# The causal mask of the transposed scores: a minimum by VectorE in the PSUM bank for a product by TensorE

## The chip, the cores and the metric

The kernel runs on one core of one Trainium2 chip. The metric is device time in microseconds (us) of one execution; less is better. The engines are named as in the profile: PE (TensorE matmul), PEld (its weight loads), DVE (VectorE), ACT (ScalarE), POOL (GpSimd) and SP (SyncE, which issues most transfers). [...]

## What is computed

A small model of six layers over `x` of 4 batches, 512 positions and 128 features, each layer added to its input:

```python
x = x + 0.5 * ffn0(layernorm(x))      # tree-routed q, k, v, one attention head of 128
x = x + attn0(layernorm(x))           # causal attention, 16 heads of 8
x = x + 0.5 * ffn0(layernorm(x))
x = x + 0.5 * ffn1(layernorm(x))      # 8 experts, 2 taken, and a shared one
x = x + attn1(layernorm(x))           # a Mamba block: a scan over the positions
x = x + 0.5 * ffn1(layernorm(x))
```

The change lies in the second layer, the attention with 16 heads:

```python
scores = jnp.einsum('bhqd,bhkd->bhqk', q, k) / math.sqrt(Dh)
scores = scores + _alibi_slopes(H)[None, :, None, None] * rel[None, None]
causal = jnp.triu(jnp.ones((S, S), dtype=bool), k=1)
scores = jnp.where(causal[None, None], jnp.float32(-1000000000.0), scores)
attn = jax.nn.softmax(scores, axis=-1)
out = jnp.einsum('bhqk,bhkd->bhqd', attn, v)
```

## The kernel before

**Jobs.** Every layer of every batch is a few Python generators, called jobs. A table of due times (`TIMES`) says when each job's steps are to be traced, and the loop at the end of `macaron` always takes the step that is due first. A list scheduler of the framework then orders the traced instructions of each engine, by that priority and by when their inputs and buffers come free in its own reckoning, and puts in all semaphores. So the order in which an engine works is fixed when the kernel is compiled, and each engine takes its instructions strictly in that order. Layers of different batches overlap: while one batch is in the 16-head attention, another is in a tree layer or with the experts.

**Buffers.** `bank(role)` takes a PSUM bank from a ring of its role (`BANKS`); `head_sc` has two, `head_max` one, `tree_mm` three. `work(role)` takes an SBUF tile from a ring (`BUFS`).

**The 16-head attention of one batch** (names starting with `head_`) runs over u = 0, 1 and g = 0, 1, four heads at a time:

- `head_prep`, `head_stack`: norm, q, k, v with the rotary embedding, written by DMA into stacks `q_bias` and `k_bias` whose extra rows carry the position bias.
- `head_keys` (L541): POOL makes four masked copies `km` of the keys, one for each head of the group.
- `head_scores`: PE makes scores with queries on the partitions (L557, bank `head_max`). One custom DVE instruction for each head (L565) takes the minimum of minus the score and the causal mask `future`, and keeps the negated row maximum. It works in place in the bank, and an accumulator read follows it.
- `head_maxima` (L579 to L584): the negated maxima are turned, split in two and written by DMA into rows of `q_bias`, so that the next product subtracts them.
- `head_mix`: scores once more, now transposed, with keys on the partitions (L633, bank `head_sc`), for one block `kt` of 128 keys and the queries from that block on: 512, 384, 256 or 128 columns for each head. A bank holds 1, 1, 2 or 4 heads, so there are 4 + 4 + 2 + 1 = 11 groups for each (u, g), and 16 x 11 = 176 groups in all. The first 128 query columns of each head meet the diagonal and need the mask. Before, this is one more product into the same bank: the identity `ident_h` as weights, and the mask `future_t` (0, or -2^100 where the key comes after the query) as moving operand, in bf16 and broadcast over the heads of the bank (L641). ACT then takes the exponential of the whole bank into a tile `pt` (L649, six tiles). Four groups later (`LAG_MIX`) PE multiplies `pt` by the values (L601, bank `head_acc`).
- `head_end`: projection and residual (L668, L669).

Other lines that the text names: `mm3` (L173 to L175) is a product of split operands in three matmuls, for the tree layers (`tree_mm`), the experts (`moe`), the scores of the tree layers' own attention (`attend`) and others; L394 is the tree layers' ReLU with the routing mask on DVE; L404 their second product; L318 a transposition on PE; L353 and L355 make the routing masks, with `leafpath` as weights; L438 is a row maximum of `attend`; L740 is part of the experts' routing; L972 is the scan of the Mamba block.

The constants are one array, `whole`, which a DMA of ACT's queue loads once at the start: `leafpath`, `ident_h`, `future_t` (128 columns each), and `future` (512 columns) for L565.

Of the kernel before, what the change touches and what calls it, by code (L numbers as in the profile page):

```python
# [17 lines left out]
BF16 = mybir.dt.bfloat16  # L18
# [3 lines left out]
ALU = mybir.AluOpType  # L22
AX = mybir.AxisListType

P = 128
B, S, D = 4, 512, 128
# [48 lines left out]
FAR = 2.0**100  # L75
# [37 lines left out]
def macaron(ctx: ExitStack, tc: tile.TileContext, t: dict, stages: int = 6):  # L113
    nc = tc.nc
# [6 lines left out]
    def bank(role):  # L121
        return psum.tile([P, S], F32, tag=role, name=role, bufs=BANKS[role])
# [4 lines left out]
    def tiny(shape, tag, bufs=2):  # L127

        n = int(np.prod(shape[1:]))
        if tag not in turns:  # L130
            first = taken_of[0]
            taken_of[0] += bufs * n
            assert taken_of[0] <= SCRATCH
            turns[tag] = cycle([scratch[:, first + n * i : first + n * i + n] for i in range(bufs)])
        out = next(turns[tag])
        if len(shape) == 2:
            return out
        names = "abcd"[: len(shape) - 1]
        sizes = dict(zip(names, shape[1:]))
        return out.rearrange(f"p ({' '.join(names)}) -> p {' '.join(names)}", **sizes)  # L140

    def work(role, shape=(S,), dtype=F32):

        return wp.tile([P, *shape], dtype, tag=role, name=role, bufs=BUFS[role])
# [19 lines left out]
    def load_split(name, src, shape, alloc_hi, alloc_lo, engine, by=None):  # L164
        raw = work("stage", shape)
        engine.dma_start(out=raw, in_=src)
        split(alloc_hi, alloc_lo, raw, by)
        return raw
# [13 lines left out]
    def keep(n):  # L182
        nonlocal cut
        cut += n
        assert cut <= KEPT
        return kept[:, cut - n : cut]
# [10 lines left out]
        rounded[:, (2 + TREES) * D + k * EXPERTS : (2 + TREES) * D + (k + 1) * EXPERTS] for k in (0, 1)  # L197
    ]
    load_split("nodes", t["nodes"], [P], *nodes, nc.scalar)
    whole = keep((3 * P + S) // 2).bitcast(BF16)  # L200
    nc.scalar.dma_start(out=whole, in_=t["whole"])
    leafpath, ident_h, future_t = (whole[:, ts(k, P)] for k in range(3))
    future = whole[:, 3 * P :]


    at = {}
# [108 lines left out]
    def transposed(src, role):  # L315
        ps = bank(role)
        for i in range(NT):
            nc.tensor.transpose(ps[:, ts(i, P)], src[:, ts(i, P)], ident)  # L318
        return ps
# [270 lines left out]
    def head_mix(b, st, consts, u, g):  # L590

        vv = consts()[2][0]
        km, qs = st.km[u, g], st.qs[u]
        if (u, g) == (0, 0):
            st.o = work("o")
        acc = bank("head_acc")

        def mix(kt, prob):
            for j in range(4):
                h = u * HALF + 2 * j + g  # L600
                nc.tensor.matmul(  # L601
                    acc[32 * j : 32 * j + 32, kt * P :],
                    lhsT=vv[:, b % 2, kt, h * (HD + 1) : h * (HD + 1) + 32],
                    rhs=prob[j],
                    start=(kt == 0),
                    stop=(kt == NT - 1),
                )

        mixed = []

        def take():
            mixed.append(work("mixed"))
            nc.scalar.copy(mixed[0], acc)

        def turn():
            ps = transposed(mixed[0], "head_turn").rearrange("p (n j c) -> p n j c", n=NT, j=4)
            rden = tiny([P, NT, 4], "rden")
            nc.vector.reciprocal(rden, ps[:, :, :, HD])
            view = st.o.rearrange("p (n u j g d) -> p n u j g d", n=NT, u=2, j=4, g=2)
            nc.vector.tensor_mul(  # L620
                view[:, :, u, :, g, :],
                ps[:, :, :, :HD],
                rden.unsqueeze(3).to_broadcast([P, NT, 4, HD]),
            )

        for kt in range(NT):
            n = S - kt * P
            prob = []
            each = (1, 1, 2, 4)[kt]
            for j0 in range(0, 4, each):  # L630
                view = bank("head_sc")[:, : each * n].rearrange("p (h k) -> p h k", h=each)
                for j in range(each):
                    nc.tensor.matmul(  # L633
                        view[:, j, :],
                        lhsT=km[(j0 + j) // 2][:, (j0 + j) % 2, ts(kt, P)],
                        rhs=qs[:, g, kt * P :],
                        start=(j == 0),
                        stop=False,
                    )

                nc.tensor.matmul(  # L641
                    view[:, :, :P],
                    lhsT=ident_h,
                    rhs=future_t.unsqueeze(1).to_broadcast([P, each, P]),
                    start=False,
                    stop=True,
                )
                pt = work("pt")[:, : each * n].rearrange("p (h k) -> p h k", h=each)
                nc.scalar.activation(pt, view, AF.Exp)  # L649
                prob += [pt[:, j, :] for j in range(each)]  # L650
                mix_later.step()
                if j0 + each == 4:
                    mix_later.add(partial(mix, kt, prob))
                    if kt == NT - 1:
                        mix_later.add(take)
                        mix_later.add(turn, 1)
                if (kt, j0) != (NT - 1, 0):
                    yield
# [508 lines left out]
def _constants():  # L1167

    f = np.float32
    leafpath = np.zeros((P, P), f)  # L1170
    leafpath[CONST_ROW, ALL_LEAVES:LEAF_LO] = 1.0
    leafpath[CONST_ROW, LEAF_LO + ALL_LEAVES :] = 1.0
    for k in range(TREES):
        for leaf in range(LEAVES):
            node = 0
            for d in range(DEPTH):
                right = leaf >> (DEPTH - 1 - d) & 1
                for base in (0, LEAF_LO):
                    leafpath[k * NODES + node, base + k * LEAVES + leaf] += -1.0 if right else 1.0
                    leafpath[CONST_ROW, base + k * LEAVES + leaf] += right  # L1180
                node = 2 * node + 1 + right

    rows = _head_rows()
    half = D // 2
    freqs = f(1.0) / f(10000.0) ** (np.arange(half, dtype=f) / f(half))
    ang = freqs[:, None] * np.arange(S, dtype=f)[None, :]
    sin, cos = np.sin(ang), np.cos(ang)
    rope = np.stack([np.concatenate([cos, cos]), np.concatenate([-sin, sin])], axis=1)[rows]

    pos = np.arange(S, dtype=np.float64)  # L1190
    q_bias = np.zeros((2, 2, R_HH, S), np.float64)
    k_bias = np.zeros((2, 2, R_HH, S), np.float64)
    for c in range(6):
        k_bias[:, :, 4 * c : 4 * c + 4] = pos if c in (0, 3) else 1.0
    for h in range(HEADS):
        u, j, g = h // HALF, h % HALF // 2, h % 2
        slope = np.float64(f(2.0 ** (-8.0 * (h + 1) / HEADS)))
        up = _rounded(slope)
        for c, part in ((0, up), (3, slope - up)):
            q_bias[u, g, 4 * c + j] = part  # L1200
            lost = -part * pos
            q_bias[u, g, 4 * (c + 1) + j] = _rounded(lost)
            q_bias[u, g, 4 * (c + 2) + j] = lost - _rounded(lost)
    row = np.arange(P)
    of_row = np.where(row < R_HH, row % 4, (row - R_HH) % 32 // HD)
    of_row[R_MAX:] = row[R_MAX:] % 4
    head = (of_row[:, None] == np.arange(4)).astype(f)

    k_after_q = np.triu(np.full((P, P), -FAR, f), 1)
    lower = np.tril(np.ones((EXPERTS, EXPERTS), f), -1)  # L1210

    gather = np.zeros((P, P), f)
    for p in range(P):
        gather[p, p // OF_GROUP] = 1.0
    spread = np.zeros((P, GROUPS, P), f)
    for q in range(GROUPS):
        for p in range(P):
            for base in (RANK, B_LOW):
                spread[base + q * OF_GROUP + p % OF_GROUP, q, p] = 1.0
    return {  # L1220
        "whole": np.concatenate(
            [leafpath, np.eye(P, dtype=f), k_after_q.T, np.zeros((P, S - P), f), k_after_q], axis=1
        ).astype(ml_dtypes.bfloat16),
        "rope": rope.astype(f),
        "q_bias": q_bias.astype(f),
        "k_bias": k_bias.astype(f),
        "lower": np.broadcast_to(lower, (P, EXPERTS, EXPERTS)),
        "state_w": np.concatenate([np.zeros((P, 6, P), f), gather.reshape(P, 1, P)], axis=1),
        "spread": spread.reshape(P, GROUPS * P),
    }, head  # L1230
# [101 lines left out]
```

## Time and profile before

| | |
|---|---|
| median of 3 runs | 1147.51 us (1146.84 to 1148.99) |
| profiled execution | 1150.85 us, span 1149.1 us |
| mean granted clock of PE | 0.988 |
| PE busy | 1080.6 us (94%), 5536 matmuls |
| PEld busy | 715.5 us (62%), 5536 loads |
| DVE busy | 909.7 us (79%), 2199 instructions |
| ACT busy | 517.1 us (45%), 1078 instructions |
| POOL busy | 411.6 us (36%), 396 instructions |

The page divides the span into 40 slices of 28.7 us; a digit is the busy share in tenths:

```
PE   3999999999999999999999999998798989998998
DVE  5566787577676777776789998799989999999864
ACT  2221423233332455544533643565476567454444
```

The lines that the change touches:

| line | what | count | busy us | mean ns |
|---|---|---|---|---|
| L633 | score product, 128 columns | 64 | 11.9 | 290 |
| L633 | score product, 256 columns | 64 | 16.0 | 331 |
| L633 | score product, 384 columns | 64 | 25.1 | 405 |
| L633 | score product, 512 columns | 64 | 29.0 | 469 |
| L641 | mask product, 128 columns | 128 | 29.4 | 230 |
| L641 | mask product, 256 columns | 32 | 9.1 | 283 |
| L641 | mask product, 512 columns | 16 | 6.2 | 389 |
| L641 | weight load of the identity | 176 | 16.9 | 96 |
| L649 | exponential, 512 columns | 112 | 64.7 | 598 |
| L649 | exponential, 384 columns | 64 | 30.4 | 492 |

[...]

### The profile page before, as it was taken

The numbers are of one execution on the slowest core, as the hardware profiler recorded it, in microseconds if no ns is written. First come the engines' busy times: TensorE is split into PE (matmuls) and PEld (weight loads), VectorE is DVE, ScalarE is ACT, GpSimd is POOL, SyncE is SP. The second block draws the span as 40 slices with busy tenths as digits, with TensorE's granted clock in tenths as the row PEclk, the third lists the DMA queues.
The fourth block names the chain that finished last, engine by engine and source line by source line (L and its number), as shares of the span: only waits on it lengthen the run. The fifth ranks groups of instructions, "written<-read, shape, count | busy, mean of one in ns | idle before, by whom it ended". The sixth has DMA issues, their size and how long they took to land.

```text
span 1149.1 us, 16519 instructions
## 1 busy us (share of the span) xinstructions
PE 1080.6 (94%) x5536; PEld 715.5 (62%) x5536; DVE 909.7 (79%) x2199; ACT 517.1 (45%) x1078; POOL 411.6 (36%) x396
## 2 busy tenths in 40 slices
PE   3999999999999999999999999998798989998998
PEld 2666566566665667765566676675276656655677
DVE  5566787577676677776789998799989999999864
ACT  2221423233332455544533643565476567454444
POOL 4115322002100141320314651266626656656623
PEclk9999999999999999999999999999899999999999
DMA  7787755231442122333752334662038323823310
GB/s 208 203 248 215 260 137 122 75 94 57 85 139 60 54 58 60 104 85 112 232 181 90 125 84 122 234 210 92 1 98 278 127 60 125 292 74 124 111 51 10
DMA packets 79653, 146.42 MB, mean 127 GB/s; under 512 B 7537, under 2 KB 39665, under 8 KB 79569
## 3 DMA queue, kind: packets, MB, share of 16 engines
q1 hardware_dynamic: 79280, 145.07, 42.1%
q8 instruction: 44, 0.72, 0.3%
q14 instruction: 41, 0.33, 0.1%
q10 hardware_dynamic: 288, 0.30, 0.1%
HBM read 125.35 MB, written 13.70 MB: 121 GB/s over the span
## 4 chain that ended last, share of the span: by engine, by line
PE 63%; DVE 20%; issue 6%; DMA 4%; POOL 3%; ACT 3%; SPq 1%; POOLq 0%; ACTq 0%; DVEq 0%
PE tree_acc L404 11%; PE moe_acc L773 7%; DVE states L972 6%; PE head_acc L601 5%; PE tree_mm L173 4%; PE head_max L557 4%; PE head_sc L633 3%; PE moe L173 3%; PE tree_mm L175 3%; PE tree_mm L174 3%; DVE states L971 3%; PE moe L174 3%; PE moe L175 3%; DVE u L759 2%; PE state_acc L934 2%
## 5 line engine op out<-in xcount | busy, mean ns | idle before, releaser
L973 POOL TENSOR_TENSOR states<-states,cs 128x512 f32<-128x512 f32 x128 | 163.4, 1282 | 161.9 <-DVE states L972 93.1
L404 PE MATMUL tree_acc<-full,ring 128*128 128x512 f32 x384 | 194.3, 598 | 5.2 <-DVE full L394 4.9
L565 DVE CUSTOM_DVE_ANT_0 head_max<-head_max,kept 128x128 f32<-128x128 f32 (+3 forms) x256 | 126.8, 496 | 64.1 <-PE head_max L557 61.9
L394 DVE SCALAR_TENSOR_TENSOR full<-tree_mm,kept,mask 128x512 f32<-128x512 f32 x188 | 138.5, 746 | 40.2 <-PE tree_mm L175 35.1
L649 ACT ACTIVATE pt<-head_sc 128x512 f32<-128x512 f32 (+1 forms) x176 | 95.0, 559 | 139.0 <-PE head_sc L641 138.3
L972 DVE TENSOR_TENSOR_SCAN states<-decay,states 128x512 f32<-128x512 f32 x128 | 154.6, 1216 | 0.5
L773 PEld LDWEIGHTS moe_acc<-ring,u 128*128 128x128 f32 x1152 | 141.4, 193 | 17.6 <-DVE u L765 3.0
L773 PE MATMUL moe_acc<-ring,u 128*128 128x128 f32 x1152 | 145.7, 278 | 1.0 <-DVE u L759 0.7
L173 PE MATMUL moe<-xl,ring 128*128 128x512 f32 x288 | 128.8, 448 | 8.9 <-DVE u L765 1.9
L784 POOL TENSOR_TENSOR kept<-kept,y 128x512 f32<-128x512 f32 x64 | 83.4, 1303 | 136.2 <-ACT y L783 118.8
L970 ACT ACTIVATE decay<-dts,kept 128x512 f32<-128x512 f32 x128 | 88.4, 693 | 88.1 <-DVE states L972 66.5
L758 ACT ACTIVATE u<-moe 128x512 f32<-128x512 f32 x144 | 86.3, 602 | 70.4 <-PE moe L175 66.5
L759 DVE SCALAR_TENSOR_TENSOR u<-u,moe 128x512 f32<-128x512 f32 x144 | 97.0, 677 | 23.4 <-ACT u L758 23.1
L174 PE MATMUL moe<-xh,ring 128*128 128x512 f32 x288 | 115.4, 401 | 0.0
L175 PE MATMUL moe<-xh,ring 128*128 128x512 f32 x288 | 115.0, 400 | 0.0
L541 POOL TENSOR_SCALAR km<-k_bias,kept 128x512 fp32r<-128x512 f32 x64 | 43.3, 697 | 171.3 <-PE head_sc L633 151.0
L783 ACT ACTIVATE y<-moe_acc,scratch 128x128 f32<-128x128 f32 x256 | 73.3, 370 | 65.6 <-PE moe_acc L773 64.8
L173 PE MATMUL tree_mm<-xl,ring 128*128 128x512 f32 x188 | 96.1, 514 | 0.4 <-DVE full L394 0.2
L404 PEld LDWEIGHTS tree_acc<-full,ring 128*128 128x128 f32 x384 | 71.0, 190 | 35.8 <-issue 17.3
L173 PEld LDWEIGHTS moe<-xl,ring 128*128 128x128 f32 x288 | 54.8, 190 | 60.4 <-DVE u L765 10.4
L557 PE MATMUL head_max<-km,q_bias 120*128 120x512 f32 (+2 forms) x192 | 91.7, 479 | 0.5 <-POOL km L541 0.4
L971 DVE TENSOR_TENSOR states<-state_b,dtxs 128x512 f32<-128x512 f32 x128 | 85.6, 682 | 5.5 <-PE state_acc L934 2.6
(242 smaller groups left out, 1982.3 us busy)
## 6 DMA issues: line engine op xcount, KB each, us to landing
ring<-moe_parts SPq DMA_DIRECT2D x72, 512.0 KB
ring<-tree_parts SPq DMA_DIRECT2D x42, 512.0 KB
ring<-in_fff_w SPq DMA_DIRECT2D x24, 512.0 KB
mask<-fff_taken SPq DMA_DIRECT2D x48, 256.0 KB
ring<-in_moe_w SPq DMA_DIRECT2D x16, 512.0 KB
dts<-state_rows SPq DMA_DIRECT2D x32, 256.0 KB
dtxs<-state_rows SPq DMA_DIRECT2D x32, 256.0 KB
moe_parts<-moe_w SPq DMA_DIRECT2D x9, 512.0 KB
```

The costliest lines, as they stand in the source:

```text
L173: nc.tensor.matmul(ps, lhsT=lh, rhs=rl, start=start, stop=False)
L174: nc.tensor.matmul(ps, lhsT=ll, rhs=rh, start=False, stop=False)
L175: nc.tensor.matmul(ps, lhsT=lh, rhs=rh, start=False, stop=stop)
L394: nc.vector.scalar_tensor_tensor(full, ps, neg_b1[:, n : n + 1], st.masks[k][:, c, :], ALU.max, ALU.mult)
L404: nc.tensor.matmul(acc, lhsT=weights[k][1][:, c, :], rhs=h, start=(c == 0), stop=False)
L557: nc.tensor.matmul(view, lhsT=qs[:R_MAX, g, ts(i, P)], rhs=km[j0 // 2][:R_MAX, j0 % 2 : j0 % 2 + each, :kw], start=True, stop=True,)
L565: nc.vector.tensor_tensor_reduce(view[:, n, :], view[:, n, :], future[:, S - kw :], -1.0, float(np.finfo(np.float32).max), ALU.add, ALU.mi ...
L759: nc.vector.scalar_tensor_tensor(u, u, 1.0, ps1, ALU.add, ALU.mult)
L773: nc.tensor.matmul(acc[:, ts(i, P)], lhsT=h[c][:, ts(i, P)], rhs=w2[:, e % 4 * 2 + c, :], start=(c == 0), stop=(c == 1),)
L971: nc.vector.tensor_mul(h, bs, dtx[:, g, :])
L972: nc.vector.tensor_tensor_scan(h, dA, h, 0.0, ALU.mult, ALU.add)
L973: nc.gpsimd.tensor_mul(h, h, cs[:, q])
```

## The change

The array `whole` loses the identity, and its mask for the transposed scores becomes `at_most`: -2^100 where the key comes after the query and 2^127 elsewhere. In `head_mix` the score products of a bank are each a group of their own (start and stop set), and the product with the identity is gone. In its place DVE takes, in the bank, the minimum of the scores' first 128 columns of each head and `at_most`, broadcast over the heads. The exponential by ACT follows as before. Lines after the change are one less in number.

```diff
-    whole = keep((3 * P + S) // 2).bitcast(BF16)
+    whole = keep((2 * P + S) // 2).bitcast(BF16)
     nc.scalar.dma_start(out=whole, in_=t["whole"])
-    leafpath, ident_h, future_t = (whole[:, ts(k, P)] for k in range(3))
-    future = whole[:, 3 * P :]
+    leafpath, at_most = (whole[:, ts(k, P)] for k in range(2))
+    future = whole[:, 2 * P :]
...
                         lhsT=km[(j0 + j) // 2][:, (j0 + j) % 2, ts(kt, P)],
                         rhs=qs[:, g, kt * P :],
-                        start=(j == 0),
-                        stop=False,
+                        start=True,
+                        stop=True,
                     )
 
-                nc.tensor.matmul(
+                nc.vector.tensor_tensor(
                     view[:, :, :P],
-                    lhsT=ident_h,
-                    rhs=future_t.unsqueeze(1).to_broadcast([P, each, P]),
-                    start=False,
-                    stop=True,
+                    view[:, :, :P],
+                    at_most.unsqueeze(1).to_broadcast([P, each, P]),
+                    ALU.min,
                 )
                 pt = work("pt")[:, : each * n].rearrange("p (h k) -> p h k", h=each)
                 nc.scalar.activation(pt, view, AF.Exp)
...
     k_after_q = np.triu(np.full((P, P), -FAR, f), 1)
+    at_most = np.where(k_after_q.T < 0, f(-FAR), f(2.0**127))
...
-            [leafpath, np.eye(P, dtype=f), k_after_q.T, np.zeros((P, S - P), f), k_after_q], axis=1
+            [leafpath, at_most, np.zeros((P, S - P), f), k_after_q], axis=1
```

## The prediction

> **What bounds the kernel now.** I read the page's totals and slices first, then sums over the stretch in which the changed line runs, then the waits in that stretch, then the timeline around single masks.
>
> The changed product is L641. Its instructions start between 134.9 and 583.8 us, so I call 130 to 585 us the head stretch. The sums by stretch (columns: us, then PE, PEld, DVE, ACT and POOL busy with instruction counts, granted clock, DMA share, GB/s):
>
> ```profile
> 130.00:585.00 455.00, 450.36 (x2454) 289.49 (x2455) 325.94 (x1034) 184.95 (x379) 87.51 (x115) 1.00 0.39 109
> 600.00:700.00 100.00, 98.56 (x515) 67.60 (x515) 97.32 (x198) 44.95 (x96) 52.93 (x47) 1.00 0.36 105
> 900.00:1000.00 100.00, 90.70 (x460) 59.27 (x458) 97.25 (x157) 63.79 (x130) 63.46 (x51) 0.98 0.44 144
> ```
>
> In the head stretch PE is busy 99% and DVE 72%; after 600 us DVE is at 97%. The two stages have different limits, and the change moves work from the first limit (PE) to the second engine, but inside the first stage only. A busy PE is not proof, because matmuls overlap, so I read who PE waits for there:
>
> ```profile
> PEld L641 <- issue: 23.2, 94, 0.5
> PEld head_max L557 <- DVE scratch L565: 4.2, 10, 0.8
> PEld head_sc L633 <- ACT pt L649: 2.3, 7, 0.6
> ```
>
> Added up over that list, weight loads wait 23.1 us for DVE, 16.0 for ACT and 2.6 for POOL; 85.2 us are "issue", time in which PE waits only for its own queue. So about 42 us of 455 are waits for others, and the rest is PE's own pace. DVE, in turn, waits for PE:
>
> ```profile
> DVE head_max L565 <- PE head_max L557: 56.4, 86, 3.1
> ```
>
> Its idle time in the stretch is 455 - 325.9 = 129 us.
>
> **What is removed from PE.** 176 identity products (busy 44.7 us) and their 176 loads (16.9 us). Busy time is not their price, because the records overlap. The price is what they add between the starts of their neighbours:
>
> ```profile
> 310.81 0.34 PE L633 MATMUL head_sc<-q_bias,km 128*128 128x384 f32 x1
> 310.99 0.10 PEld L641 LDWEIGHTS <-kept 128*128 128x128 bf16 x1 [0.22 <-issue]
> 310.99 0.23 PE L641 MATMUL head_sc<-kept 128*128 128x128 bf16 x1
> 311.03 0.48 PE L173 MATMUL attend<-tree_k,tree_q 128*128 128x512 f32 x1
> 311.35 0.39 PE L174 MATMUL attend<-tree_k,tree_q 128*128 128x512 f32 x1
> ...
> 311.81 0.40 PE L173 MATMUL tree_mm<-xl,ring 128*128 128x512 f32 x1
> 312.04 0.39 PE L174 MATMUL tree_mm<-xh,ring 128*128 128x512 f32 x1
> ```
>
> From L633 to L174 it takes 0.54 us here. Without a mask, L173 to L174 takes 0.23 (last two lines) and a 384-wide product frees PE after about 0.18: 0.41, so this mask costs 0.13. Over the whole head stretch I took the same gap for every neighbour. A 512-wide product, the mask and an L173/L174 pair: median 594.5 ns over 8, without the mask 467 over 37: 128 ns. Before L175/L404: 595 to 465. Before two L404: 881 to 663. Before L601, whose 32-wide f32 loads don't follow at once either: 446 to 387, 408 to 438, 591 to 574, in the mean 15 ns. The instruction that follows L641 in the compiled order is L601 in 49 cases, a split (fp32r) product in 98, L318 in 16, L404 in 6, another in 7. So 98 x 0.13 + 49 x 0.02 + 16 x 0.07 + 6 x 0.20 + 7 x 0.10 = 12.7 + 1.0 + 1.1 + 1.2 + 0.7 = **17 us** (0.07 for L318 and 0.10 for the rest are chosen between 0 and 0.2). Lower bound: the 39 ns from a mask's start to that of a following L173, 176 times, 7 us. Upper bound: the whole busy time, 45 us. I take 17 because it comes from the same neighbours.
>
> [...]
>
> **What is added on DVE.** 176 minima in place in the PSUM bank: 128 of 128x128 (one head in the bank), 32 of 128x256, 16 of 128x512. The nearest rows also write PSUM in place with an operand from `kept`:
>
> ```profile
> L565 DVE CUSTOM_DVE_ANT_0 head_max<-head_max,kept 128x512 f32<-128x512 f32 x64 | 44.6, 697 | 26.8 <-PE head_max L557 26.3
> L565 DVE CUSTOM_DVE_ANT_0 head_max<-head_max,kept 128x128 f32<-128x128 f32 x64 | 18.8, 294 | 8.6 <-PE head_max L557 8.0
> L740 DVE TENSOR_TENSOR moe_tr<-moe_tr,kept 128x256 f32<-128x256 f32 x8 | 3.4, 420 | 0.0
> ```
>
> 128 x 0.29 + 32 x 0.42 + 16 x 0.70 = 37.1 + 13.4 + 11.2 = **61.7 us busy**. DVE in the stretch goes to 325.9 + 61.7 = 388 of some 450 us, 86%. The cover is its 129 us of idle time; with the cover gone all 61.7 would be on the path. Successive DVE records overlap (an L565 of 128x128 is followed by the next start after a median 215 ns, not 294), so the engine's own time is nearer 128 x 0.21 + 32 x 0.34 + 16 x 0.60 = 47 us.
>
> [...]
>
> **What waits longer.** Score, mask and exponential of a group now run PE, DVE, ACT, each a semaphore apart, in one of two head_sc banks.
>
> ```profile
> L649 ACT ACTIVATE pt<-head_sc 128x512 f32<-128x512 f32 x112 | 64.7, 598 | 99.3 <-PE head_sc L641 98.7
> ```
>
> Before, a bank is held from the mask's issue for 0.23 + 0.05 + 0.60 + 0.05 = 0.9 us (0.05 being the step from one engine's end to the next start, as from 300.66 to 300.70 in the timeline). Now from the last score's issue: 0.17 (what remains of its 0.40) + 0.05 + 0.29 + 0.05 + 0.60 + 0.05 = 1.2 us, plus the wait in DVE's queue. I priced the PE work that lies between a group and the next one in its bank, in the compiled order of each kernel, by the gaps of the trace (0.23 for 512-wide, 0.11 for 128-wide, 0.43 for L404). Before, 23 of 174 reuses have less than 1.0 us, and are short by some 3.5 us in all at 0.9. In the changed order 32 have less than 1.5 us and are short by 12.6; at 2.0 us 34.6. DVE's wait I take as 0.3 us: at 86% load, with operations of 0.3 to 0.75 us, a mask finds one of them half done. That is 1.5 us held: 12.6 - 3.5 = **9 us of new PE waits**. The bounds are 0 (no queue, 4.9 - 3.5) and 61.7 (all of the masks exposed).
>
> On DVE each mask stands ahead of L565 (which frees the single head_max bank for L557), L394 and L438. Of PE's 23.1 us of waits for DVE, a growth by 61.7/326 = 19% would be 4 us; half of it belongs to L565 and counts: **2 us**. What follows in L601 has cover: it comes four groups later (LAG_MIX).
>
> **Edits at nothing.** The `whole` load shrinks from 224 KB to 192 KB, 0.15 us at the 208 GB/s of the first slice, hidden: L353, its first reader, starts at 18.6 us, after `small` and two norms. Start and stop flags issue nothing. No DMA is moved past a queue, and the work in each queue between landmarks stays (DVE has 1166 instructions up to the last L565 before, 1325 now), so after 585 us the same work runs, shifted.
>
> **Sum.** Against the profiled execution's 1150.85 us (span 1149.1): -17 + 9 + 2 = -6, 1144.85. The median of the runs is 3.34 below that execution, so 1147.51 - 6 = **1141.5 us**.
>
> **The rivals.**
> *DVE's queue paces the banks (slower).* Place: the two head_sc banks. If a mask waits 0.8 us on DVE in place of 0.3, banks are held 2.0 us: -17 + (34.6 - 3.5) + 4 = +18, 1165.5. It decides from about 0.6 us of wait, where the shortage reaches 19 us. For it: DVE at 86%, L394 takes 0.75 us and L565 0.84 with its read. Against: in the changed order only 24 of 176 masks stand behind a DVE instruction whose product PE issues later; and the 97% after 600 us, beside a PE at 98.6%, shows that DVE can run so full.
> *No new wait.* The masks fit in the 129 us: -17 to -20, 1129. For it: DVE idles mostly on L557. Against: 32 tight reuses.
> *The gain is not passed on.* PE ends the heads 6 us sooner, but the scans (first at 567.3 us, DVE at 97%) wait for something else, and the end stays: 1147.5. Against: their input comes through the same batches.
>
> **How the numbers follow.** Forecast 0.40, no new wait 0.12, not passed on 0.10, DVE's queue 0.38. The measurement tells about 0.2%, 2.3 us. Of the forecast 0.04 ends within that; of the third rival 0.06 does, with 0.02 on either side: faster 0.36 + 0.12 + 0.02 = 0.50, same 0.10, slower 0.38 + 0.02 = 0.40. The range for 8 in 10 reaches from below the second rival, whose PE price may be 24 in place of 17, to the slower one's price: 1124 to 1166. The forecast's own range is 1130 to 1146.
>
> **What would show it.** L641 as a DVE row of 0.29, 0.42 and 0.70 us; L633 followed at once by L173 after 0.23 us; the head stretch ending some 6 us earlier, at 579; PE waits of L633 for L649 at about 11 us. Wrong if L633's waits pass 20 us, or if the first scan starts after 567.

## The result, and the profile after

| | before | after |
|---|---|---|
| median of 4 runs | 1147.45 us (1146.84 to 1148.99) | 1157.79 us (1155.6 to 1159.84) |
| span of the profiled execution | 1149.1 us | 1156.0 us |

The ratio is 1.0088, with a 95% interval of 1.0067 to 1.0109: the change makes the kernel slower by 10 us, where 6 us less were forecast. The two profiled executions are 6.9 us apart only, because that of before took 3.4 us more than its median: readings from the traces show some 7 of the 10 us.

The page of the kernel after, totals and slices:

```profile
span 1156.0 us, 16358 instructions
PE 1078.1 (93%) x5360; PEld 709.5 (61%) x5360; DVE 951.2 (82%) x2375; ACT 518.6 (45%) x1078; POOL 411.0 (36%) x396
PE   3999989999999989999999999998798989988998
DVE  5566788778787788877789998799999999989864
```

The 176 products are gone and the 176 minima are there (5536 to 5360 on PE, 2199 to 2375 on DVE). PE's slices hardly differ; DVE's digits rise by one in most slices of the head stretch, by two in one of them, and none reaches 9 there. The sums of the kernel after over the three stretches shown of before (us, then PE, PEld, DVE, ACT, POOL busy with counts, clock, DMA share, GB/s):

```profile
130.00:585.00 455.00, 441.20 (x2233) 279.14 (x2233) 360.44 (x1188) 185.04 (x377) 87.23 (x115) 1.00 0.38 105
600.00:700.00 100.00, 98.63 (x528) 66.88 (x526) 97.50 (x184) 46.04 (x97) 51.30 (x43) 1.00 0.37 104
900.00:1000.00 100.00, 93.07 (x491) 61.86 (x490) 97.02 (x163) 64.27 (x133) 61.72 (x50) 0.98 0.40 126
```

After 600 us the stages look as before. In the head stretch PE is busy 9 us less, and still the stretch ends later, not sooner. DVE is at 79% there and not full, and PE, at 97% against 99%, is idle more than before: the reason has to be in who waits for whom. The waits of the kernel after between 130 and 590 us (us in all, times, longest):

```profile
ACT pt L648 <- DVE head_sc L641: 120.3, 82, 5.6
DVE head_max L565 <- PE head_max L557: 36.9, 63, 2.5
...
PEld tree_mm L173 <- DVE full L394: 4.3, 5, 2.0
...
PEld head_acc L601 <- ACT pt L648: 3.8, 3, 2.1
...
PEld head_sc L633 <- ACT pt L648: 2.8, 7, 0.6
```

L633 waits 2.8 us for the exponential that frees its head_sc bank, against 2.3 before. Over all that released them, the weight loads of L633 wait 9.4 us against 4.4 ("issue" left out). Of the 9 us more that were forecast there 5 came, and next to nothing of that at the exponential. DVE waits less for PE (36.9 against 56.4), because it is itself the later one. Added up over the whole list, weight loads wait 32.8 us for DVE (before 23.3), 23.8 for ACT (16.8) and 5.3 for POOL (2.6).

**Where the time goes.** I matched the instructions that both kernels have, line by line and in order, and took how much later each starts than in the kernel before: the median over PE, DVE and ACT within 8 us of a position. This is worked out from the traces, and another way of matching moves single values by up to 1 us; columns are positions in the time of before, in us:

```
                125   170   240   340   388   432   485   520   545   640  1130
after           1.4   7.0   3.3   0.2  -2.8   2.9   3.3   9.4   7.8   6.8   7.0
none            0.8   2.6  -1.0  -3.8  -5.9  -3.3  -5.9  -5.9  -6.0  -6.8  -6.0
both            0.9   8.9   9.2   8.3   7.5  13.4  14.8  18.9  18.7  18.8  21.5
pool            0.8   3.3  -0.3  -2.9  -5.0  -3.7  -4.9  -4.6  -4.9  -5.6  -8.8
touch           1.4   7.5   5.1   2.6  -0.7   1.8   1.9   2.1   1.5   1.4   2.1
after_hm2       1.0  10.7   7.1   1.9  -2.0   3.4   1.9   2.3   2.0   0.6   0.4
mixed_steady    1.5   1.0  -2.6  -5.7  -7.3  -7.0  -7.0  -6.7  -6.6  -6.7  -4.9
```

(The other rows are kernels of the experiments below.) The first row falls and rises. From 170 to 388 us the kernel after gains 9.8 us, in the direction of the forecast. It loses 5.6 us from 125 to 170, 5.7 from 388 to 432 and 6.1 from 485 to 520. The last is in part another order: near 520 the heads' scores, maxima and exponentials are late by 9 to 11 us, while the tree layers' L404 starts 2.6 us early, and at 545 4.5 us of the loss are left. After 545 the lag is only carried along. The three losses lie where batches go over from one layer to the next: DVE then has the norms of the next layer and the tree layers' L394 in the queue where the minima now stand.

**The first loss**, in the timeline of the kernel after (start, duration, engine, line, operation; in brackets the idle time before it and its releaser):

```profile
155.66 0.28 DVE L284 BATCH_NORM_STATS2 scratch<-kept 128x6 f32<-128x128 f32 x1
155.86 0.36 DVE L286 BATCH_NORM_AGGREGATE scratch<-scratch 128x2 f32<-128x6 f32 x4
156.14 0.40 DVE L565 CUSTOM_DVE_ANT_0 head_max<-head_max,kept 128x256 f32<-128x256 f32 x1
...
157.27 0.41 PE L557 MATMUL head_max<-km,q_bias 120*128 120x384 f32 x1 [1.43 <-DVE scratch L271]
...
158.67 2.07 DVE L394 SCALAR_TENSOR_TENSOR full<-tree_mm,kept,mask 128x512 f32<-128x512 f32 x3
159.48 0.80 PE L173 MATMUL tree_mm<-xl,ring 128*128 128x512 f32 x1 [1.79 <-DVE full L394]
...
160.07 0.63 PE L174 MATMUL tree_mm<-xh,ring 128*128 128x512 f32 x1
...
160.50 0.63 PE L175 MATMUL tree_mm<-xh,ring 128*128 128x512 f32 x1
```

The same step in the kernel before:

```profile
154.15 2.07 DVE L394 SCALAR_TENSOR_TENSOR full<-tree_mm,kept,mask 128x512 f32<-128x512 f32 x3
...
154.96 0.50 PE L173 MATMUL tree_mm<-xl,ring 128*128 128x512 f32 x1 [0.22 <-DVE full L394]
```

DVE works through a backlog of small norm operations and of L565 without a pause (busy 5.00 of 5.00 us from 155 to 160). PE waits 1.43 and 1.79 us, and the three L394 come at 158.67 in place of 154.15, 4.5 us late, of which 1.4 us was there when the heads began. No minimum stands in these lines. Ten stand ahead of them, from 136 to 150 us, and the norms come in another order than in the kernel before. That the minima pushed the queue back isn't shown here, for DVE is idle in 3.1 of the 5 us from 140 us on. It is the kernels below that tie the loss to them: `touch` has it as well, `none` and `pool` have less than half of it, `mixed_steady` has none.

**The second loss** shows the minimum itself on the path. The chain of waits of the kernel after (start, us, engine and line):

```profile
417.40 0.64 ACT head_k L514
418.04 0.02 issue
418.06 0.69 DVE head_k L515
418.76 0.22 DVE head_sc L641
418.97 0.02 issue
419.00 0.50 ACT pt L648
419.50 0.04 issue
419.54 0.83 PE head_acc L601 x2
```

and of the kernel before, with the same work of the rotary embedding:

```profile
416.25 0.63 ACT head_k L514
416.88 0.49 ACT vv L520
417.37 0.04 issue
417.41 1.05 PE head_acc L601 x2
```

In the kernel after, the minimum's score ended at 416.01 us and the minimum starts at 418.67, 2.66 us later: L515 stands ahead of it in DVE's order and waits for ACT's L514, DVE idling 0.48 us, and ACT had idled 1.94 us until POOL's L511 ended. So the mask waits for other keys than its own, and exponential and L601 with it; PE idles 1.76 us where it idled 1.08. The larger part follows: PE then idles 0.93, 0.71 and 1.16 us between 424 and 430 us. The small operations of the experts' norm, which stood between 415.5 and 420.3 us on DVE before, now run from 423.3 to 426.5 us, behind and among minima: that is another order of DVE's instructions, not the old one delayed. Added up over the chain from 130 to 600 us, PE holds 437.6 us before and 393.4 after, DVE 9.6 and 41.5, ACT 7.3 and 16.9. Of the 437.6, L641 had 15.3. Of DVE's 41.5, the minima themselves have only 3.3: the rest is other work of DVE that they made late, or that came to the top once PE's part was shorter.

### The profile page after: what moved, and what is told of

Its sections match the earlier page's. It is cut to its first block, busy times and chain, and to the rows that moved or that the text cites. A ratio compares the mean times of both kernels' runs of the same rounds, so it can differ in the third digit from the quotient of the medians.

```text
span 1156.0 us, 16358 instructions
## 1 busy us (share of the span) xinstructions
PE 1078.1 (93%) x5360; PEld 709.5 (61%) x5360; DVE 951.2 (82%) x2375; ACT 518.6 (45%) x1078; POOL 411.0 (36%) x396
## 4 chain that ended last, share of the span: by engine, by line
PE 60%; DVE 21%; issue 6%; DMA 5%; POOL 4%; ACT 3%; SPq 1%; POOLq 0%; ACTq 0%; DVEq 0%
PE tree_acc L404 11%; DVE states L971 6%; PE moe_acc L772 6%; PE head_acc L601 5%; PE tree_mm L173 4%; PE moe L173 3%; PE head_max L557 3%; PE head_sc L633 3%; PE moe L174 3%; DVE states L970 3%; PE moe L175 3%; PE tree_mm L174 3%; PE tree_mm L175 3%; PE state_acc L933 2%; DVE u L758 2%
## 5 line engine op out<-in xcount | busy, mean ns | idle before, releaser
L404 PE MATMUL tree_acc<-full,ring 128*128 128x512 f32 x384 | 194.1, 599 | 5.6 <-DVE full L394 5.1
L565 DVE CUSTOM_DVE_ANT_0 head_max<-head_max,kept 128x128 f32<-128x128 f32 (+3 forms) x256 | 126.3, 493 | 46.2 <-PE head_max L557 42.4
L394 DVE SCALAR_TENSOR_TENSOR full<-tree_mm,kept,mask 128x512 f32<-128x512 f32 x188 | 138.2, 744 | 31.0 <-PE tree_mm L175 21.9
L648 ACT ACTIVATE pt<-head_sc 128x512 f32<-128x512 f32 (+1 forms) x176 | 95.6, 559 | 141.5 <-DVE head_sc L641 125.9
L173 PE MATMUL moe<-xl,ring 128*128 128x512 f32 x288 | 128.5, 447 | 10.1 <-DVE states L971 2.3
L782 ACT ACTIVATE y<-moe_acc,scratch 128x128 f32<-128x128 f32 x256 | 73.5, 369 | 62.6 <-PE moe_acc L772 61.7
L173 PE MATMUL tree_mm<-xl,ring 128*128 128x512 f32 x188 | 94.7, 506 | 3.1 <-DVE full L394 2.2
L404 PEld LDWEIGHTS tree_acc<-full,ring 128*128 128x128 f32 x384 | 70.7, 190 | 38.3 <-issue 20.0
L557 PE MATMUL head_max<-km,q_bias 120*128 120x512 f32 (+2 forms) x192 | 90.9, 474 | 3.0 <-DVE scratch L271 1.4
L173 PEld LDWEIGHTS moe<-xl,ring 128*128 128x128 f32 x288 | 54.7, 190 | 61.4 <-DVE u L764 10.9
```

The lines of the kernel that those rows point to most:

```text
L173: nc.tensor.matmul(ps, lhsT=lh, rhs=rl, start=start, stop=False)
L394: nc.vector.scalar_tensor_tensor(full, ps, neg_b1[:, n : n + 1], st.masks[k][:, c, :], ALU.max, ALU.mult)
L404: nc.tensor.matmul(acc, lhsT=weights[k][1][:, c, :], rhs=h, start=(c == 0), stop=False)
L557: nc.tensor.matmul(view, lhsT=qs[:R_MAX, g, ts(i, P)], rhs=km[j0 // 2][:R_MAX, j0 % 2 : j0 % 2 + each, :kw], start=True, stop=True,)
L565: nc.vector.tensor_tensor_reduce(view[:, n, :], view[:, n, :], future[:, S - kw :], -1.0, float(np.finfo(np.float32).max), ALU.add, ALU.mi ...
```

## The experiments

As the experiments are told in groups, the expectations don't stand in the order of the runs, and some speak of results of earlier ones. Three explanations were set against each other. The first (theory A in the expectations): the price is the minima's work and place in DVE's queue, at the handovers between layers. The second (C): the head_sc banks, the place that the prediction named. The third (B): the list scheduler's order, which any edit changes. Ratios are to the kernel before on the same chip, with 95% intervals. The kernel after itself is 1.0088 [1.0067, 1.0109].

**Each half alone.** `none` has no mask at all, `both` has the product and the minimum:

```diff
 none
-                nc.vector.tensor_tensor(view[:, :, :P], view[:, :, :P], at_most..., ALU.min)
-                nc.scalar.activation(pt, view, AF.Exp)
+                nc.scalar.activation(pt, view, AF.Exp, scale=2.0**-6)
 both
+                nc.tensor.matmul(view[:, :, :P], lhsT=ident_h, rhs=future_t..., start=False, stop=True)
                 nc.vector.tensor_tensor(view[:, :, :P], view[:, :, :P], at_most..., ALU.min)
```

> The changed kernel without the DVE minimum: no mask at all (so the attention sees later keys; the exponential gets a scale of 2^-6 to stay finite, which changes no instruction count). Theory A, the minima overload DVE at the places where a batch passes from one layer to the next and PE idles there: without them the whole PE saving shows, 1147.5 - 17 - about 3 = 1128 to 1134 us, and PE does not stand idle for 3 us near 156. Theory B, the loss comes from the scheduler's new order and not from DVE's time: this kernel is reordered just as much, so 1140 to 1158 us. Theory C, three engines in a row hold the two head_sc banks: also fast here, 1128 to 1134, so A and C are not told apart by this run.

Measured: 0.9957 [0.9942, 0.9973], a median of 1145.1 us. That lies in the range of theory B, the order, and not in that of A and C: the whole PE saving doesn't show.

> The identity product on PE is kept and the DVE minimum is added behind it (the mask is applied twice, 64 more columns of constants). Theory A: the DVE time without the saving on PE, 1157.8 + 17 = 1170 to 1178 us. Theory B: the added minima cost little by themselves and only the order decides, 1142 to 1165. If the effects of the two parts add up, none + both - before = the changed kernel's 1157.8.

Measured: 1.0193 [1.0178, 1.0207], 1171.8 us, in theory A's range. Taking the product away is worth 0.43% (before to none, 5 us) or 1.05% (both to after, 12 us). The minimum costs 1.31% (none to after, 15 us) or 1.93% (before to both, 22 us). Along either way the sum is the change: -5 + 15 or +22 - 12, +10 us. So the forecast saving is partly there, and the minimum costs more than it brings. In the chain of `none`, from 130 to 600 us, DVE holds 38.9 us with no minimum at all: with PE's part gone, other work comes to the top. So 15.3 us of L641 on the path bring only 5, and DVE's 41.5 us in the chain of after are no measure of the minima.

**The same work on another queue.** `pool` masks with POOL after the exponential, in the SBUF tile `pt`:

```diff
-                nc.vector.tensor_tensor(view[:, :, :P], view[:, :, :P], at_most..., ALU.min)
-                nc.scalar.activation(pt, view, AF.Exp)
+                nc.scalar.activation(pt, view, AF.Exp, bias=-40.0)
+                nc.gpsimd.affine_select(pt[:, :, :P], pt[:, :, :P], [[0, each], [1, P]],
+                    ALU.is_ge, 0.0, base=0, channel_multiplier=-1)
```

> The mask is taken off PE and DVE: POOL sets the later keys to zero in the SBUF tile after the exponential (which gets a bias of -40 that cancels in the quotient). The bank goes PE, ACT and is free. Theory A: PE saves 17 us and DVE has nothing more to do, 1128 to 1138 us, unless POOL's records of the added operation pass 0.6 us each or its queue holds up L601. Theory B: 1140 to 1158. Theory C: 1128 to 1138.

Measured: 0.9969 [0.9957, 0.9981], 1145.6 us, within 0.12% of `none`, and like it in theory B's range. POOL's groups there, by form:

```profile
L643 POOL TENSOR_SCALAR_AFFINE_SELECT pt<-pt 128x128 f32<-128x128 f32 x128 | 38.0, 301 | 151.4 <-ACT pt L642 149.2 <-DMA k_bias<-head_k 1.4
...
L643 POOL TENSOR_SCALAR_AFFINE_SELECT pt<-pt 128x256 f32<-128x256 f32 x32 | 13.1, 409 | 60.5 <-ACT pt L642 57.7 <-DVE full L394 2.2
```

One takes 301 or 409 ns, about what DVE's minimum takes (307 and 431). What differs is the queue: POOL is busy 41% of the span with the masks (36% without), and sits idle until the exponential ends. The place differs too: after the exponential the PSUM bank is free already, so this run alone doesn't separate the two.

**DVE's time or DVE's queue.** `touch` leaves each minimum in its place but only one column wide for each head, so that most of the mask is left out:

```diff
-                    view[:, :, :P],
-                    view[:, :, :P],
-                    at_most.unsqueeze(1).to_broadcast([P, each, P]),
+                    view[:, :, :1],
+                    view[:, :, :1],
+                    at_most[:, :1].unsqueeze(1).to_broadcast([P, each, 1]),
```

> The minimum on DVE shrunk to one column for each head (so the mask is left out in effect; scale 2^-6 in the exponential as in the kernel with no mask): the step through DVE, its semaphores and its place in DVE's queue stay, its time goes from 0.29 to 0.70 us down to about 0.1. If the price of the minima (13 to 15 us at HEAD_LAG 0.39, between 0.9957 with no mask and 1.0088) is DVE's time, most of it goes: ratio 0.996 to 1.000. If it is the added step (a bank and a group of exponentials that wait in DVE's queue behind whatever stands there), most of it stays: 1.004 to 1.009.

Measured: 1.0033 [1.002, 1.0046], between the two ranges. The minima of `touch`, by line (count, then min, median and max ns):

```profile
L641 DVE TENSOR_TENSOR head_sc<-head_sc,kept x176: 141/168/210, 136.4 to 586.1; 128x1 f32<-128x1 f32 x128, 128x2 f32<-128x2 f32 x32, 128x4 f32<-128x4 f32 x16
```

Of the 1.31% from none to after, 0.76 stay with 128 times fewer columns (some 0.2 either way). The first loss is there in full (7.5 us of lag at 170), the second shrinks to 2.5, the third to next to nothing. But a step of 0.14 to 0.21 us still takes time: DVE is busy 924.2 us in all, against 908.6 in `none` and 951.2 in after, so 15.6 of the 42.6 us that the minima add are left, 37%. The price falls to 58%, which is hardly more than its noise above 37%. So at this lag the run doesn't tell DVE's time from the place in its queue.

**Buffers.** A second bank for head_max, a third for head_sc:

```diff
-BANKS = dict(..., head_max=1, ..., head_sc=2, ...)
+BANKS = dict(..., head_max=2, ..., head_sc=2, ...)    after_hm2, before_hm2
+BANKS = dict(..., head_max=1, ..., head_sc=3, ...)    after_sc3
```

> The changed kernel with three head_sc banks. Theory C (the prediction's: the masks' wait on DVE holds the two head_sc banks): the 9 us and more that I had put there come back, ratio to before 0.999 to 1.002. Theory A (DVE's time, by way of head_max, tree_mm and the norms): no gain, 1.006 to 1.011. Theory B (order): either.

Measured: 1.0078 [1.0057, 1.0099], in theory A's range and the same as after within the intervals. A third bank takes away what the prediction held to be the price, and nothing comes back: the head_sc banks are not the place.

> The changed kernel with two head_max banks in place of one. Theory A, in the form that DVE's backlog reaches PE through the single head_max bank (1.4 us idle before an L557 at 155.8): part of it comes back, 1149 to 1154 us. Theory C (head_sc): no change, 1156 to 1160. Theory B: anywhere within 1148 to 1165.

Measured: 1.0012 [1.0003, 1.0022], 1150.7 us, in the ranges of A and B, not in C's.

> The kernel before (mask by PE) with two head_max banks: the control to the changed kernel with two banks, which came to 1.0012 of before, against 1.0088 with one bank. If the second bank helps because it lifts the wait that the minima on DVE bring (theory A by way of head_max), it does little here: ratio 0.998 to 1.002. If it helps any kernel of this kind, or by its order alone, it is as much faster here: ratio 0.990 to 0.995.

Measured: 1.004 [1.0025, 1.0055], slower than either range. With a second head_max bank the kernel after loses the third handover's lag (2.3 us at 520 in place of 9.4), not the first's, while the kernel before gets slower. The bank itself is no gain, then, and the single head_max bank seems to pass a good part of DVE's delay on to PE; with two, the change comes out 0.28% ahead. But the second bank brings a new order too, which alone can be worth as much (next group), so this isn't shown.

**Another order.** A different lag of the heads in the due times makes the scheduler order everything anew:

```diff
-HEAD_LAG = 0.39
+HEAD_LAG = 0.42
```

> The kernel before with the same shift of the order. It tells how much an order is worth with nothing else changed: theory A 0.998 to 1.003; theory B up to 1.010 slower, because any other order would be slower than this one.

Measured: 1.0058 [1.0043, 1.0073], in theory B's range.

> The changed kernel with the transposed scores traced a little later (HEAD_LAG 0.42 in place of 0.39): the same instructions in another order. Theory A: as the changed kernel, ratio to before 1.006 to 1.012. Theory B: the order is worth some 10 us by itself, so it may fall anywhere from 0.997 to 1.015.

Measured: 1.0063 [1.0046, 1.0079], which both ranges hold. In this order the change costs 0.05%, that is nothing that can be told. Its halves were run there as well:

> No mask at all (scale 2^-6 in the exponential), HEAD_LAG 0.42. With the two kernels at 0.42 (1.0058 with PE's mask, 1.0063 with DVE's) it gives the price of each mask in another order. Theory A, that DVE's minima cost some 13 us whatever the order: 1.0063 - 0.011 = 0.995 (0.993 to 0.997). Theory B, that the sizes of both parts are those of an order: anywhere from 0.995 to 1.006.

Measured: 0.9894 [0.9877, 0.9911], faster than either range.

> Both masks, HEAD_LAG 0.42. Theory A: the kernel before at 0.42 and the minima, 1.0058 + 0.013 to 0.019 = 1.019 to 1.025. Theory B: 1.006 to 1.025, and less than 1.012 would say that the minima themselves cost little in this order.

Measured: 1.0207 [1.0191, 1.0224], which both ranges hold.

> The same at HEAD_LAG 0.42, where no mask is 0.9894 and the whole minimum 1.0063. DVE's time: 0.990 to 0.995. The added step: 1.001 to 1.006.

Measured: 1.0054 [1.0038, 1.007], in the range of the added step.

> The mask on POOL after the exponential (0.9969 at HEAD_LAG 0.39), at 0.42. If taking the mask off both PE and DVE is a gain of its own, it is faster than both kernels at 0.42 too, by about as much as at 0.39: 1.000 to 1.004. If the gain was one of order, 1.004 to 1.008 or more.

Measured: 0.9958 [0.9946, 0.997], faster than either range, and 0.64% above its own `none`. All ratios together:

| lag | product | none | minimum | both | touch | pool |
|---|---|---|---|---|---|---|
| 0.39 | 1 | 0.9957 | 1.0088 | 1.0193 | 1.0033 | 0.9969 |
| 0.42 | 1.0058 | 0.9894 | 1.0063 | 1.0207 | 1.0054 | 0.9958 |

The product costs 0.43 to 1.64% over the four pairs, the minimum 1.31 to 1.93%. In the second order 0.0160 of the minimum's 0.0169 stay in `touch`, while of the 42.3 us that the minima add to DVE's busy time 17.3 are left: there the price hardly follows DVE's time, and the place in the queue is almost all of it. What swings is the net, from -0.28 to +0.88%, because the product costs little beside `none` at 0.39 with one bank, and more at 0.42. With the mask unchanged, a new order moves the time by 0.4 to 0.6% (before_hm2, before_lag42; `none` to `none_lag42` by as much the other way). The measured +0.88% is the minimum's 1.31% less the product's 0.43, and each of them holds order in that measure.

**Minima only where they cost nothing.** If the losses lie at the handovers, minima in the steady stretch alone must gain. `mixed01` has them in batches 0 and 1 (the last starts at 358 us), `mixed_steady` leaves out the first half of batch 0 as well (its first starts at 187 us); the product stays elsewhere:

```diff
+                if b < 2:                                        mixed01
+                if (b, u) in ((0, 1), (1, 0), (1, 1)):           mixed_steady
                     nc.vector.tensor_tensor(view[:, :, :P], ..., ALU.min)
+                else:
+                    nc.tensor.matmul(view[:, :, :P], lhsT=ident_h, ..., start=False, stop=True)
```

> The minimum by DVE in the attention of batches 0 and 1 (masks up to about 390 us), the product by PE in batches 2 and 3. In the changed kernel's trace the lag behind the kernel before goes from +6.8 us at 175 to -3.0 us at 395 and then up to +9 us at the handovers near 410 to 430 and 500 to 515. Theory A (the minima cost where DVE also has the norms of a handover): what is gained up to 390 stays and the later loss goes, ratio to before 0.994 to 0.999. Theory B (order): anywhere between 0.996 and 1.008.

Measured: 1.0002 [0.9992, 1.0013], above theory A's range and within that of B. Its lag is flat from 388 on, as expected, but at -1.9 us only: the loss from 125 to 170 (6.4 us of lag) was kept.

> The minimum by DVE only for the second half of batch 0's heads and for batch 1 (masks from about 185 to 390 us), the product by PE elsewhere. In every kernel with all minima the lag behind the kernel before grows by 4 to 9 us between 135 and 170 us and by 5 to 9 between 390 and 435, and falls by 8 to 12 between. Theory A (cost at the handovers): the rise at 135 to 170 goes as well and the fall stays, so 3 to 7 us faster than before: ratio 0.994 to 0.998. If the fall is only the making up of what was lost at 135 to 170, 0.999 to 1.002.

Measured: 0.9957 [0.9941, 0.9973], in theory A's range, some 5 us less than before, and faster than both kernels. The lag at 170 is 1.0 us, at 388 it is -7.3. The two kernels differ in 22 minima at the first handover, and in the order that follows from them; these turn a gain of 0.43% into none. With `pool_lag42` it is the fastest kernel here that computes the whole.

## Why the prediction was wrong

The range holds the time, but only because it reaches up to the slower rival's 1165.5, whose place was wrong too; the sign is wrong. The forecast was -17 + 11 = -6 us. The halves measured -5 + 15 (the product taken away first) or +22 - 12 (the minimum added first). Of the 16 us between forecast and result, 12 or 5 lie in PE's saving and 4 or 11 in what waits longer, so both terms failed. Step by step:

- **PE's saving, -17 us:** right in mechanism, too large for this order. A score product now frees PE at once, as was forecast (the kernel after, 0.23 us from start to start):

```profile
300.87 0.40 PE L633 MATMUL head_sc<-q_bias,km 128*128 128x512 f32 x1
...
301.10 1.02 PE L404 MATMUL tree_acc<-full,ring 128*128 128x512 f32 x2
```

  The halves give 5 and 12 us at 0.39, and 19 and 17 at 0.42. The chain of before has 15.3 us of L641. The estimate priced PE's own time, which comes near what the other order gives; it didn't ask what is next on the path when that time is gone.
- **61.7 us of DVE records, 47 of own time:** right. By form, in the kernel after:

```profile
L641 DVE TENSOR_TENSOR head_sc<-head_sc,kept 128x128 f32<-128x128 f32 x128 | 38.5, 307 | 12.2 <-PE head_sc L633 11.6
...
L641 DVE TENSOR_TENSOR head_sc<-head_sc,kept 128x256 f32<-128x256 f32 x32 | 13.6, 431 | 4.2 <-PE head_sc L633 3.5 <-ACT pt L648 0.7
...
L641 DVE TENSOR_TENSOR head_sc<-head_sc,kept 128x512 f32<-128x512 f32 x16 | 11.2, 699 | 0.0
```

  The mean ns are 307, 431 and 699 against 290, 420 and 700; 63.3 us of records, while DVE's total rose by 951.2 - 909.7 = 41.5. Where an instruction follows at once, it starts 0.21, 0.33 or 0.60 us after the minimum in the median, as forecast.
- **The cover, "its 129 us of idle time":** this step failed, and the waits below were sized by it. The sum over 455 us is true, but at the handovers there is little idle time. At the first one DVE was nearly full already in the kernel before (its busy time is the third of the sums):

```profile
150.00:155.00 5.00, 4.08 (x39) 2.22 (x37) 4.67 (x30) 1.18 (x2) 0.00 (x0) 1.00 1.11 205
155.00:160.00 5.00, 5.00 (x19) 3.26 (x20) 4.69 (x19) 0.60 (x1) 1.73 (x4) 1.00 0.07 10
```

  In the kernel after it is busy 5.00 of 5.00 us from 155 to 160 us. In the steady stretch the cover held: 9.8 us gained.
- **"DVE's wait I take as 0.3 us":** mis-sized, since it came from the mean load. From a score's end to the start of its minimum it is 0.88 us in the mean from 130 to 172, 0.62 from 172 to 388, 1.11 from 388 to 436, and 0.61 to 0.63 until 545. The 0.62 us of the steady stretch, twice the forecast, cost nothing there: it matters where the wait falls. With L515 ahead it isn't even all a wait for work: of the 2.66 us from the score's end to the minimum DVE idles 0.48, in its strict order.
- **"9 us of new PE waits" at the head_sc banks:** wrong place. For the exponential that frees the bank L633 waits 0.5 us more, over all releasers 5 us, and a third bank brings nothing back. (The lower bound there, 4.9 - 3.5, is 1.4 us and not 0.) In the traces above the path went by L394 to L173, by L565's single bank to L557, by L648 to L601, and by the norms.
- **"2 us" for L565 and L557, and L601's cover of four groups:** too small. PE's waits for DVE grew by 9.5 us, and the single head_max bank seems to bear on the third handover (after_hm2). L601 waits for L648 up to 2.1 us: four groups are no cover when several exponentials are late together, three of them behind L515 in the second loss.
- **After 585 us "the same work runs, shifted":** right, 7.8 us at 545 and 7.0 at 1130; the first scan starts at 574.3 in place of 567.3, which the prediction had named as a sign of being wrong.
- **The slower rival** had the sign and a wait above its 0.6 us, but named the head_sc banks, so its 1165.5 is no hit either. "Not passed on" falls with the first scan; "no new wait" comes near from 170 to 388 us alone.

The rows were right on the overlap, yet in `touch` 176 operations of one column, 0.14 to 0.21 us each, still cost 0.76 to 1.60% of the time.

Still open: how much of the 10 us is chance of this order, and, at this lag, how the minimum's price divides into DVE's time and the place in its queue. The scheduler orders anew with each edit, so no run holds the order fixed; a second order and a second bank show the range, not the share. `pool` comes nearest to a fixed order: against `none`, 79 of DVE's 2199 instructions stand at another place, where between before and after 689 do (the minima left out).

## What to carry to other kernels

A step put into DVE's strict order was paid here in delay to what stands behind it (7.0 us of lag at 170 us with all minima, 1.0 without those of the first handover), and waited for what stands ahead (2.66 us behind L515): cover is to be read stretch by stretch, at the handovers above all, not from the mean idle time of a stage. A shorter operation need not make such a step cheap (one column for 128 left 0.76 of 1.31% in one order and 1.60 of 1.69% in the other); a queue that idles until the work comes (POOL's here, after the exponential: 0.9969 and 0.9958) or a stretch where the queue has slack (the steady one here: 0.9957) did. Where a scheduler orders the code, measure each half of a change in more than one order before the net is believed.

## What the runs showed of the hardware

After the waits at 155.8 to 159.5 us PE runs at half clock. The sums of the kernel after there (columns as above; the clock is the third number from the end):

```profile
155.00:160.00 5.00, 1.77 (x9) 0.87 (x4) 5.00 (x36) 0.00 (x0) 0.00 (x0) 0.89 1.14 187
160.00:165.00 5.00, 5.00 (x19) 3.47 (x17) 4.00 (x13) 0.89 (x2) 2.82 (x5) 0.76 0.00 0
```

The clock is half from 158.9 us for 3.41 us, and the split products, shown above, start 0.43 us apart in place of 0.23. In the 3.41 us ahead of 158.9 us PE was idle for 2.7, in two pieces with a product between. Of the time at half clock PE worked 2.9 us, which by these distances cost it some 1.4 us (an estimate). The other half-clock times of the two kernels last 3.41 or 6.83 us and move from kernel to kernel (among them 799.9, 820.4 and 936.5 us before; 807.5, 828.0 and 944.0 after, some 7.6 us later with the lag). From 100 us to the end of the work, PE was busy for 0.21 to 0.56 of the 3.41 us ahead of each of the ten halvings in these two traces. Laid end to end from there, the stretches of 3.41 us at full clock that no half clock followed have PE busy for 0.59 or more, but for one of 0.48. So the half clock came after stretches with PE busy for up to 0.56, and not after the one of 0.48; the 3.41 us are the length of the shorter half-clock times, and what sets the clock no run shows.
